# Second bias of 48 experts: spread over partitions ahead of the loop and added by VectorE, with token gathers issued an expert ahead

## The chip, the core and the metric

The kernel runs on one core of a Trainium2 chip. The core has five engines with queues of their own: PE (TensorE, matmuls and transposes), DVE (VectorE), ACT (ScalarE), POOL (GpSimd) and SP (SyncE, which here issues DMAs only). The metric is the device time of one execution in microseconds (us); of several runs the median is given.

## The reference, cut to what matters

The program is four layers deep, and each layer has an attention part and a feed-forward part. The change lies in the second layer's feed-forward part, a mixture of 48 experts over 4096 tokens of 256 numbers. Each expert picks the 128 tokens with its highest scores out of the 4096 tokens; the batch is 8 sequences of 512.

```python
E, S, D, M = (48, 4, 256, 256)
K = D // S
...
logits = xf @ Wr.T
vals, idx = jax.lax.top_k(logits.T, cap)          # cap = 128
w = jax.nn.softmax(vals, axis=-1)
xg = xf[idx]
h = jax.nn.gelu(jnp.einsum('ecd,esdm->ecsm', xg, W1) + b1[:, None], approximate=False)
y = jnp.einsum('ecsm,esmk->ecsk', h, W2) + b2[:, None]
y = y.reshape(E, cap, D) * w[..., None]
out = jnp.zeros_like(xf).at[idx.reshape(-1)].add(y.reshape(-1, D))
```

`b2` is the second bias: one row of 256 numbers for each expert, the same for all of its 128 tokens.

## The kernel before, in words

Activations stay in SBUF as `X`, 8 sequences of 4 x 128 tokens with the tokens on partitions. The part in question is the function `l1_ffn` (line 1326 on); it follows `l1_attn` and uses the helper class `Choice`.

**The gap.** The routing of seven sequences is done during the attention part. What is left when the attention of the eighth sequence ends can't be hidden. `finish` of `l1_attn` ends with the output projection (L193), its norm (`stats`, L105 to L96, and L170 on DVE, L177 on ACT) and the addition to `X` (L182 on POOL). Then `ch.logits(7)` takes the norm of that sequence (L105 to L133, DVE), stores it in DRAM (`xn_d`, L1156), transposes it (L146), copies it (L148) and multiplies by the router's weights (L1165, L1170). `ch.lists(4)` sorts: 16 rounds of MAX8, FIND_INDEX8 and MATCH_REPLACE8 on DVE (L1183 to L1188), and stores the table (L1195, SP). `ch.slots` merges all lists on DVE, reads windows of the table with five indirect DMAs (L1277, POOL) and ends with the tokens' indices `iT` and weights `wT` for all experts.

**The loop.** For each expert `e`: SP loads `w1` (1 MB, L1350), `w2` (256 KB, L1351) and the row `b2` (1 KB, L1352), each with three buffers; POOL gathers the 128 tokens (L1354, two buffers); PE transposes them (L1359) and DVE copies them to `xgT` (L1361). PE multiplies by `w1` (L1368, 32 instructions, since each float32 matmul is two), ACT takes the gelu with the first bias (L1373, 8 instructions). The second stage accumulates in one PSUM tile `py`: first a matmul of a row of ones with the row `b2` (L1377, two instructions), which puts the bias on all 128 rows, then eight matmuls of 64 columns (L1379, 16 instructions) on top of it. DVE weights the result (L1383), and POOL adds it to the tokens' rows in DRAM with an indirect DMA (L1384).

**The order.** Each engine works through its queue in order and waits at an instruction until what it needs is there. The order of each queue is fixed when the program is built, by the framework's own estimate of when things are ready; it need not be the order of the text. So the profile has the transposes L1359 and the bias matmul L1377 of the next expert between the L1379 of this one, and weight loads of the first three experts ahead of the table's store on SP.

Of the kernel before, what the change touches and what calls it, by code (L numbers as in the profile page):

```python
# [9 lines left out]
F32 = mybir.dt.float32  # L10
# [4 lines left out]
ALU = mybir.AluOpType  # L15
# [4 lines left out]
P = 128  # L20
NB = 8
L = 512
NT = 4
D = 256
# [1080 lines left out]
class Choice:  # L1105
# [7 lines left out]
    E, NL, K = 48, 10, 128  # L1113
# [212 lines left out]
def l1_ffn(K):  # L1326
    nc, tc = K.nc, K.tc
    b1 = K.W["l1_ffn"][:, 96:480]
    ch, i = K.choice, K.i
    E = ch.E  # L1330
    with ExitStack() as es:
        es.enter_context(ch.es)

        def pool(name, bufs, **kw):
            return es.enter_context(tc.tile_pool(name="f1" + name, bufs=bufs, **kw))
        cst = pool("c", 1)
        wp = pool("w", 3)
        sb = pool("s", 2)
        pmm = pool("pm", 2, space=PSUM)
        pH = pool("ph", 4, space=PSUM)  # L1340
        pY = pool("py", 2, space=PSUM)
        ch.logits(NB - 1, sb, pmm, "mm")
        for _ in ch.lists(len(ch.GROUPS) - 1):
            pass
        wT, iT = ch.slots(cst, sb, pmm, "mm")
        for e in range(E):
            w1 = wp.tile([P, 4, 2, D], F32, tag="w1", name=f"w1_{e}")
            w2 = wp.tile([P, 4, 2, 64], F32, tag="w2", name=f"w2_{e}")
            b2 = wp.tile([1, D], F32, tag="b2", name=f"b2_{e}")
            nc.sync.dma_start(out=w1, in_=i["l1f_w1"][e].rearrange("s (c p) m -> p s c m", p=P))  # L1350
            nc.sync.dma_start(out=w2, in_=i["l1f_w2"][e].rearrange("s (c p) k -> p s c k", p=P))  # L1351
            nc.sync.dma_start(out=b2, in_=i["l1f_b2"][e:e + 1, :])  # L1352
            xg = sb.tile([P, D], F32, tag="xg", name=f"xg{e}")
            nc.gpsimd.indirect_dma_start(  # L1354
                out=xg, out_offset=None, in_=ch.xn_d[:, :],
                in_offset=bass.IndirectOffsetOnAxis(ap=iT[:, e:e + 1], axis=0))
            ps = pmm.tile([P, 2, P], F32, tag="mm", name=f"pxg{e}")
            for c in range(2):
                nc.tensor.transpose(ps[:, c, :], xg[:, c * P:(c + 1) * P], K.ident)  # L1359
            xgT = sb.tile([P, 2, P], F32, tag="xgT", name=f"xgT{e}")  # L1360
            nc.vector.tensor_copy(xgT, ps)  # L1361
            hT = sb.tile([P, 8, P], F32, tag="hT", name=f"hT{e}")
            for half in range(2):
                ph = pH.tile([P, 4, P], F32, tag="h", name=f"h{e}_{half}")
                for j in range(4):
                    s, m = 2 * half + j // 2, j % 2
                    for c in range(2):
                        nc.tensor.matmul(  # L1368
                            ph[:, j, :], lhsT=w1[:, s, c, m * P:(m + 1) * P],
                            rhs=xgT[:, c, :], start=(c == 0), stop=(c == 1))  # L1370
                for j in range(4):
                    q = 4 * half + j
                    nc.scalar.activation(  # L1373
                        hT[:, q, :], ph[:, j, :], AF.Gelu,
                        bias=b1[:, 8 * e + q:8 * e + q + 1])
            py = pY.tile([P, D], F32, tag="y", name=f"y{e}")
            nc.tensor.matmul(py, lhsT=K.ones, rhs=b2, start=True, stop=False)  # L1377
            for q in range(8):
                nc.tensor.matmul(  # L1379
                    py[:, (q // 2) * 64:(q // 2 + 1) * 64], lhsT=hT[:, q, :],  # L1380
                    rhs=w2[:, q // 2, q % 2, :], start=False, stop=(q == 7))
            yw = sb.tile([P, D], F32, tag="yw", name=f"yw{e}")
            nc.vector.tensor_scalar(yw, py, wT[:, e:e + 1], None, ALU.mult)  # L1383
            nc.gpsimd.indirect_dma_start(  # L1384
                out=ch.out_d[:, :],
                out_offset=bass.IndirectOffsetOnAxis(ap=iT[:, e:e + 1], axis=0),
                in_=yw, in_offset=None, compute_op=ALU.add)

    def late(b, pool):
        y = pool.tile([P, NT, D], F32, tag="xn", name=f"yl{b}")  # L1390
        nc.sync.dma_start(
            out=y, in_=ch.out_d[b * L:(b + 1) * L].rearrange("(n p) d -> p n d", p=P))
        K.add_norm(b, [y[:, n, :] for n in range(NT)], pool, parts=2)


    K.late = late
# [847 lines left out]
def l3_ffn(K):  # L2244
# [18 lines left out]
    with ExitStack() as es:  # L2263
# [295 lines left out]
        for b in range(NB):  # L2559
# [11 lines left out]

LAYERS = (("l0_attn", load_l0_attn, l0_attn), ("l0_ffn", load_l0_ffn, l0_ffn),
          ("l1_attn", load_l1_attn, l1_attn), ("l1_ffn", load_l1_ffn, l1_ffn),
          ("l2_attn", load_l2_attn, l2_attn), ("l2_ffn", load_l2_ffn, lambda K: None),
          ("l3_attn", load_l3_attn, l3_attn), ("l3_ffn", lambda K: None, l3_ffn))
# [94 lines left out]
```

## Time and profile before

| what | value |
|---|---|
| median of 3 runs | 4563.06 us (4558.62 to 4568.67) |
| profiled execution | 4555.24 us |
| its span, first to last instruction | 4553.5 us |
| mean granted PE clock | 0.93 of full speed |
| PE busy | 3963.8 us, 87% of the span |
| DVE busy | 2698.8 us, 59% |
| POOL busy | 2118.9 us, 47% |
| ACT busy | 2016.2 us, 44% |
| end of the last L193 of the attention to the first L1359 of the experts | 1513.8 to 1577.1 us |
| first L1359 to the last L1383 of the experts | 1577.1 to 1882.0 us |

How to read the lines: a line of the timeline has the start and the duration in us, the engine, the line of the source, the operation, the output and the inputs by the program's names, partitions x elements, and how many instructions were merged into it; in brackets stands how long the engine was idle before and what ended that. Buffer numbers are left out of names, so `y` is `y0`, `y1` and so on. PEld is PE's loading of weights, which lies beside its matmuls. SPq is an instruction that only issues a DMA. The clock is a share of full speed.

### The profile page before, as it was taken

Reading aid. Unit: us, or ns where it says so; the run is one execution under the profiler, and the core shown is the slowest. Engines: PE = TensorE matmul, PEld = TensorE weight load, DVE = VectorE, ACT = ScalarE, POOL = GpSimd, SP = SyncE. Lnnn points to the kernel's source line nnn. Section 1 sums busy time; section 2 is a strip of 40 time slices with the busy share of each in tenths; the row PEclk is TensorE's granted clock in tenths of the full one; section 3 lists DMA queues with packets and bytes.
Section 4 is the critical chain, followed back from the end, with each engine's and each line's share of the span. In section 5 each row is a group of like instructions: output and inputs, shape, how many; then the busy total and the mean of one; then the engine's idle time right before and its main releaser. Section 6 shows DMA issues by size and latency. Waiting matters only on the chain. (4 is left out here: it accounts for less than half of the span.)

```text
span 4553.5 us, 63426 instructions
## 1 busy us (share of the span) xinstructions
PE 3963.8 (87%) x21672; PEld 2633.7 (58%) x21672; DVE 2698.8 (59%) x7145; ACT 2016.2 (44%) x4210; POOL 2118.9 (47%) x2081
## 2 busy tenths in 40 slices
PE   8868888999998599699999978998888876899997
PEld 3435765555655499544554534565655545678884
DVE  7767656456757611255566534888888899721115
ACT  5532433444344233334444444767676655311112
POOL 0045222444344244344555423889988879223321
PEclk9889999999999799889999989899999886899999
DMA  4377621000000299400000002343433334336653
GB/s 120 94 218 189 179 62 63 5 5 7 7 10 16 69 254 251 130 5 10 6 6 6 1 23 68 123 125 126 127 122 122 124 110 136 103 118 234 228 180 113
DMA packets 392818, 442.90 MB, mean 97 GB/s; under 512 B 147853, under 2 KB 275967, under 8 KB 391983
## 3 DMA queue, kind: packets, MB, share of 16 engines
q1 hardware_dynamic: 361087, 390.18, 28.4%
q0 software_dynamic: 16272, 31.87, 2.6%
q10 hardware_dynamic: 15136, 16.80, 1.1%
q8 instruction: 172, 2.82, 0.3%
q14 instruction: 151, 1.24, 0.1%
HBM read 372.49 MB, written 66.26 MB: 96 GB/s over the span
## 5 line engine op out<-in xcount | busy, mean ns | idle before, releaser
L2085 POOL TENSOR_TENSOR h<-h,C 128x1024 f32<-128x1024 f32 x256 | 613.3, 2408 | 135.3 <-DVE h L2081 87.8
L2081 DVE TENSOR_TENSOR_SCAN h<-dA,dB 128x512 f32<-128x512 f32 x480 | 568.4, 1209 | 90.2 <-ACT dA L2069 73.9
L1039 POOL TENSOR_SCALAR p<-p,rs 128x128 f32<-128x128 f32 (+3 forms) x256 | 275.8, 1085 | 417.3 <-DVE rs L1038 261.1
L2069 ACT ACTIVATE dA<-dl,A 128x512 f32<-128x512 f32 x480 | 330.3, 690 | 174.4 <-DVE h L2081 173.7
L1605 DVE CUSTOM_DVE_ANT_0 junk<-S,mask 128x256 f32<-128x256 f32 (+3 forms) x512 | 249.5, 487 | 195.0 <-PE S L1599 156.7
L2098 PE MATMUL y<-C,h 128*128 128x128 f32 x2048 | 298.4, 297 | 68.0 <-POOL h L2085 67.9
L2098 PEld LDWEIGHTS y<-C,h 128*128 128x128 f32 x2048 | 263.2, 155 | 155.3 <-POOL h L2085 98.6
L1633 ACT ACTIVATE PT<-T 128x128 f32<-128x128 f32 (+3 forms) x512 | 198.0, 435 | 278.5 <-PE T L1628 267.6
L1599 PE MATMUL S<-KZ,QT 64*128 64x512 f32 (+3 forms) x1024 | 260.9, 492 | 23.9 <-DVE mx L1605 23.6
L2297 PE MATMUL gb<-xbT,w_b 128*128 128x256 f32 (+1 forms) x1472 | 255.3, 332 | 1.0 <-ACT ts L2501 0.6
L2297 PEld LDWEIGHTS gb<-xbT,w_b 128*128 128x128 f32 x1472 | 230.4, 191 | 22.8 <-ACT ts L2501 0.8
L2303 DVE TENSOR_TENSOR hTb<-sb,gb 128x512 f32<-128x512 f32 x71 | 48.8, 687 | 325.4 <-PE gb L2297 325.4
L2064 POOL TENSOR_TENSOR dB<-du,B 128x1024 f32<-128x1024 f32 x96 | 234.0, 2437 | 0.1
L1883 PE MATMUL pf<-fT,w_l_ffn 128*128 128x512 f32 x384 | 208.3, 681 | 26.5 <-ACT fT L1877 10.4
L1628 PE MATMUL T<-QT,KZ 64*128 64x384 f32 (+3 forms) x1024 | 216.7, 464 | 2.9 <-ACT PT L1633 2.5
L2064 DVE TENSOR_TENSOR dB<-du,pb 128x1024 f32<-128x1024 f32 x160 | 191.2, 1195 | 23.0 <-ACT pb L2062 21.2
L182 POOL TENSOR_TENSOR X<-X,yn 128x256 f32<-128x256 f32 (+1 forms) x56 | 79.4, 1436 | 255.3 <-ACT yn L177 213.9
L1373 ACT ACTIVATE hT<-h,w_l_ffn 128x128 f32<-128x128 f32 x384 | 109.5, 368 | 197.9 <-PE h L1368 197.9
L1368 PE MATMUL h<-xgT,w 128*128 128x128 f32 x1536 | 185.0, 279 | 0.0
L1636 POOL TENSOR_SCALAR_AFFINE_SELECT PT<-PT 128x512 f32<-128x512 f32 x128 | 81.2, 634 | 219.8 <-ACT PT L1633 206.8
L1599 PEld LDWEIGHTS S<-KZ,QT 64*128 64x128 f32 x1024 | 117.2, 193 | 113.9 <-issue 58.4
L2534 POOL DMA_INDIRECT ys<-yb,place x71 | 69.8, 984 | 238.7 <-ACT yb L2533 224.5
(605 smaller groups left out, 9266.5 us busy)
## 6 DMA issues: line engine op xcount, KB each, us to landing
w_b<-l3f_w SPq DMA_DIRECT2D x138, 512.0 KB
C<-xdd SPq DMA_DIRECT2D x256, 256.0 KB
B<-xdd SPq DMA_DIRECT2D x256, 256.0 KB
w<-l1f_w SPq DMA_DIRECT2D x48, 1024.0 KB
w<-l1f_w SPq DMA_DIRECT2D x48, 256.0 KB
band<-l0fd SPq DMA_DIRECT2D x30, 320.0 KB
X<-x SPq DMA_DIRECT2D x16, 512.0 KB
c<-ys SPq DMA_DIRECT2D x16, 512.0 KB
```

The source lines that it names most:

```text
L1039: nc.gpsimd.tensor_scalar(p[:, 0:n], p[:, 0:n], rs, None, ALU.mult)
L1599: nc.tensor.matmul(ps[:, 0:n], lhsT=QT[half, qt * P:n], rhs=KZ[half, j % 2, 0:n], start=True, stop=True)
L1605: nc.vector.tensor_tensor_reduce(out=junk[:, 0:n], in0=ps[:, 0:n], in1=mask[:, L - n:L], scale=1.0, scalar=-3.0e38, op0=ALU.add, op1=ALU.m ...
L1628: nc.tensor.matmul(ps[:, 0:n], lhsT=KZ[half, j % 2, kt * P:(kt + 1) * P], rhs=QT[half, kt * P:L], start=True, stop=True)
L1633: nc.scalar.activation(PT[:, j, :], ps[:, 0:n], AF.Exp)
L1883: nc.tensor.matmul(ps, lhsT=gu[:, k, j * 768 + c * P:j * 768 + (c + 1) * P], rhs=R[b]["fT"][:, k, :], start=(k == 0), stop=(k == 1))
L2064: on.tensor_tensor(dBs[k], R[b]["du", h], B[:, None, :].to_broadcast([P, 2, L]), ALU.mult)
L2069: nc.scalar.activation(dA, R[b]["dl", h][:, c, :], AF.Exp, scale=A[:, 2 * h + c, n:n + 1])
L2081: nc.vector.tensor_tensor_scan(hs[k][:, c, :], dA, dBs[k][:, c, :], 0.0, ALU.mult, ALU.add)
L2085: nc.gpsimd.tensor_tensor(hs[k], hs[k], row_C.pop(k)[:, None, :].to_broadcast([P, 2, L]), ALU.mult)
L2098: nc.tensor.matmul(R[b]["y", h][q // 2][:, q % 2, c * P:(c + 1) * P], lhsT=t[:, c, q * P:(q + 1) * P], rhs=K.ident, is_transpose=True, sta ...
L2297: nc.tensor.matmul(ps[:, q, :], lhsT=ww[:, k, (c + q) * P:(c + q + 1) * P], rhs=xT[:, k, :], start=(k == 0), stop=(k == 1))
```

## The change

The second bias leaves the accumulation. In the gap all 48 rows are loaded with experts on partitions (48 x 256). For each pair of experts POOL multiplies the rows with two columns of the identity, which leaves only the own row of each expert in a block of 48 x 512; a matmul with a 48 x 128 tile of ones sums over the 48 rows and so puts the pair's rows on all 128 partitions, and ACT copies them to the tile `bb` in SBUF (48 KB on each partition). The scratch for the product takes the buffers of `w2`. In the loop the eight matmuls start their own sums, and DVE adds `bb` before it weights. The gather of expert `e + 1` is now issued, in the text, before the work on expert `e`, with three buffers instead of two. `ch.logits` of the last sequence takes its tiles from a pool that is closed again before the loop.

```diff
-        ch.logits(NB - 1, sb, pmm, "mm")
+        bb = cst.tile([P, E, D], F32, name="bb")
+        with ExitStack() as eg:
+            sg = eg.enter_context(tc.tile_pool(name="f1g", bufs=1))
+            b2 = sg.tile([E, D], F32, name="b2")
+            nc.sync.dma_start(out=b2, in_=i["l1f_b2"])
+            ch.logits(NB - 1, sg, pmm, "mm")
+            one = sg.tile([E, P], F32, name="one")
+            nc.gpsimd.memset(one, 1.0)
+            for e in range(0, E, 2):
+                own = wp.tile([P, 4, 2, 64], F32, tag="w2", name=f"own{e}")
+                own = own[0:E].rearrange("p a b k -> p (a b k)").rearrange("p (m d) -> p m d", m=2)
+                nc.gpsimd.tensor_tensor(
+                    own, b2[:, None, :].to_broadcast([E, 2, D]),
+                    K.ident[0:E, e:e + 2, None].to_broadcast([E, 2, D]), ALU.mult)
+                pb = pH.tile([P, 2, D], F32, tag="h", name=f"pb{e}")
+                nc.tensor.matmul(pb, lhsT=one, rhs=own, start=True, stop=True)
+                nc.scalar.copy(bb[:, e:e + 2, :], pb)
...
+        xgs = {}
+
+        def gather(e):
+            xgs[e] = sb.tile([P, D], F32, tag="xg", name=f"xg{e}", bufs=3)
+            nc.gpsimd.indirect_dma_start(
+                out=xgs[e], out_offset=None, in_=ch.xn_d[:, :],
+                in_offset=bass.IndirectOffsetOnAxis(ap=iT[:, e:e + 1], axis=0))
+
+        gather(0)
         for e in range(E):
...
-            b2 = wp.tile([1, D], F32, tag="b2", name=f"b2_{e}")
...
-            nc.sync.dma_start(out=b2, in_=i["l1f_b2"][e:e + 1, :])
-            xg = sb.tile([P, D], F32, tag="xg", name=f"xg{e}")
-            nc.gpsimd.indirect_dma_start(
-                out=xg, out_offset=None, in_=ch.xn_d[:, :],
-                in_offset=bass.IndirectOffsetOnAxis(ap=iT[:, e:e + 1], axis=0))
+            if e + 1 < E:
+                gather(e + 1)
+            xg = xgs.pop(e)
...
-            nc.tensor.matmul(py, lhsT=K.ones, rhs=b2, start=True, stop=False)
             for q in range(8):
                 nc.tensor.matmul(
                     py[:, (q // 2) * 64:(q // 2 + 1) * 64], lhsT=hT[:, q, :],
-                    rhs=w2[:, q // 2, q % 2, :], start=False, stop=(q == 7))
+                    rhs=w2[:, q // 2, q % 2, :], start=(q % 2 == 0), stop=(q % 2 == 1))
             yw = sb.tile([P, D], F32, tag="yw", name=f"yw{e}")
-            nc.vector.tensor_scalar(yw, py, wT[:, e:e + 1], None, ALU.mult)
+            nc.vector.tensor_tensor(yw, py, bb[:, e, :], ALU.add)
+            nc.vector.tensor_scalar(yw, yw, wT[:, e:e + 1], None, ALU.mult)
```

## The prediction

> **What bounds the kernel now.** I read the page first and found no one bound: the engines' shares change from stage to stage. So I went to the two stages that the change touches, by a table of windows (the columns after the window's length are PE, PEld, DVE, ACT and POOL busy with instruction counts, granted clock, DMA share, GB/s), then the timeline in each, then the waits.
>
> ```profile
> 1514.00:1577.00 63.00, 11.54 (x40) 8.94 (x39) 43.93 (x182) 8.68 (x18) 9.65 (x11) 0.56 0.14 41
> ...
> 1650.00:1700.00 50.00, 50.00 (x415) 46.38 (x414) 6.98 (x16) 18.24 (x64) 20.34 (x16) 1.00 0.95 249
> ```
>
> The first line is the gap: routing of the last sequence, one chain that runs mostly on DVE; PE, ACT, POOL and the DMA are nearly idle. The second is the expert loop: PE is never idle, at full clock. So in the gap only what delays DVE's chain costs, and in the loop only PE's queue counts. The timeline of one loop period shows that queue:
>
> ```profile
> 1722.47 1.23 PE L1379 MATMUL y<-w,hT 128*128 128x64 f32 x10
> 1722.66 0.37 SPq L1350 DMA_DIRECT2D w<-l1f_w  x1
> 1722.67 1.14 ACT L1373 ACTIVATE hT<-h,w_l_ffn 128x128 f32<-128x128 f32 x4 [0.58 <-PE h L1368]
> ...
> 1723.53 0.28 PE L1359 MATMUL pxg<-C,xg 128*128 128x128 f32 x1
> ...
> 1723.82 0.28 PE L1359 MATMUL pxg<-C,xg 128*128 128x128 f32 x1
> ...
> 1724.02 0.69 PE L1377 MATMUL y<-b,ones 1*128 1x256 f32 x2
> 1724.13 0.42 DVE L1361 COPY xgT<-pxg 128x256 f32<-128x256 f32 x1 [4.60 <-PE pxg L1359]
> ...
> 1724.65 0.66 PE L1379 MATMUL y<-w,hT 128*128 128x64 f32 x4
> ...
> 1725.14 3.79 PE L1368 MATMUL h<-xgT,w 128*128 128x128 f32 x32
> ```
>
> Read: the transposes of the next expert's tokens and its bias matmul (L1377) already stand among this expert's y matmuls. h starts at 1605.40, 1611.70, 1618.01 and so on: a period of 6.30 us.
>
> **Part 1, the bias matmul leaves the loop.** L1377 holds PE from 1724.02 to 1724.65, when the next y starts: 0.63 us. Without it the last four y instructions run 1724.02 to 1724.51 (their 0.49 us). What is late next is xgT: its copy starts when the second transpose ends and is done at 1724.13 + 0.42 = 1724.55. With a hop of about 0.07 (estimate; the copy itself starts 0.03 after the transposes) h starts at 1724.62 and not 1725.14: 0.52 us per expert. The gelu does not bind: its last four end at 1723.81, before the y matmuls that read them. 47 periods x 0.52 = **24.4 us gained**. From above it is the whole 0.63: 29.6 us. From below it is less than nothing, if the build orders PE's queue otherwise (rival C).
>
> Could the DMA, at 0.95, become the bound? Its share is not flat: in slices of 0.3 us it carries w1 at about 380 GB/s, then w2 at 180 to 290, and falls to 0.06 to 0.6 for some 1.5 us of each period. The prefetch of three experts ran in 12.7 us (1504.7 to 1517.4), 4.2 us each; gather and scatter come on top, 1.44 us per expert if the software queue's 18.0% of 16 engines in 1500 to 1885 is put end to end. That is 5.7 at most, against a period of 5.78. It stays hidden.
>
> **Part 2, DVE's added instruction.** y is read from PSUM by an addition (nearest: 128x256 of L889, two operands and one of them PSUM, 0.42) and then weighted from SBUF (L133's 0.35), in place of 0.48. DVE has 7 us of work in 50, and the scatter has slack: POOL waits 3 us per period. So nothing in the loop, some 0.3 us once behind the last expert, and 0.3 for reordered starts: +0.6.
>
> **Part 3, the gather an expert ahead.** At 1604.63 the gather is issued right after the transposes that freed its buffer; with two buffers that is already the tokens of two experts on, used 11 us later, and it lands in 4.2 us. PE waited for a gather twice in all, 4.1 us, at the start. Gain: nothing. The 48 loads of one row that leave SP's queue freed nothing anyone waited for.
>
> **Part 4, the spreading in the gap.** Added: a load of 48 KB, a memset, 24 POOL products of 48x512, 24 pairs of matmul instructions of 512 columns, 24 ACT copies of 128x512. ACT: 24 x 0.58 = 13.9 us beside 8.7 busy in 63. PE: L193 does 256 columns in 0.22, so 24 x 2 x 0.44 = 21 us beside 11.5 busy. POOL: rows with a spread operand of 512 are L1587 at 1.04 and L1547 at 1.06, plain ones reach 1.27 (L1498) and 1.43 (L672); I take 1.1, so 24 x 1.1 = 26 us of POOL, idle from 1521 to the window gathers at 1564. By room alone all is free. The weights' buffers w2 serve as scratch, so w2 loads wait for the last product; even from 1550 on three experts' weights land in 12.7 us, before 1577, and the table store at 1553.29 has until 1564.
>
> But POOL and DVE are not independent:
>
> ```profile
> 748.01 2.35 POOL L182 TENSOR_TENSOR X<-X,yn 128x1024 f32<-128x1024 f32 x1 [6.00 <-ACT yn L177]
> 748.13 2.25 DVE L96 SCALAR_TENSOR_TENSOR ony<-onw,ony 128x4 f32<-128x4 f32 x1
> ```
>
> and, earlier, with two POOL products in a row:
>
> ```profile
> 446.99 1.27 POOL L903 TENSOR_TENSOR oT<-oT,ro 128x512 f32<-128x512 f32 x1 [0.34 <-ACT ro L901]
> 447.23 1.57 DVE L906 SCALAR_TENSOR_TENSOR oT<-sq,oT 128x512 f32<-128x512 f32 x1
> 448.21 2.80 POOL L762 TENSOR_TENSOR bq<-bq,PQ 128x1024 f32<-128x1024 f32 x1
> ```
>
> A 0.16 us DVE instruction on 128x4 takes 2.25 and ends with POOL's product, 20 ns after it. In the second view DVE's turn comes when POOL's instruction ends, and POOL's next one is longer. So while POOL runs products back to back, each DVE instruction with two SBUF inputs passes once per product. MAX8, FIND_INDEX8, BATCH_NORM_STATS2 and the like never stretched.
>
> Which are exposed: the root of the output norm (L94 to L96 three times each, L170: 10, at 1515.5 to 1517.4), that of the routing norm (9, at 1522.3 to 1524.0) and the four L133 (1524.1 to 1525.5; L133's longest is 2.46, so it is held too). Products can't start before the bias rows are in and PSUM is free; L1377 of the first experts ran at 1513.77, so I start there. Some three products go before X's additions, which interrupt POOL until about 1521; about 18 are left, 20 us in a row, over the whole second chain. 13 exposed instructions x (1.1 - 0.2) = 11.7; for the first chain 3 x 0.9 = 2.7, taken at half, 1.3, since the start is uncertain. Transposes and copies of the chain queue behind the spreading's own on PE and ACT: +1. In return PE is kept warm: the clock was 0.50 from 1518.75 to 1528.5 and L1165 took 3.03 for 8 instructions of 256 columns, 1.8 at L193's pace, and the 8 transposes would give some 0.8: -2. **Gap: 11.7 + 1.3 + 1 - 2 = +12.** Lower end -2 (products fall under the 20 us of MAX8 and its like); upper end 28 (24 products of 1.27 each charged, less 24 x 0.2, and two more ahead of X's additions).
>
> [...]
>
> **Sum** on the profiled execution (4555.24, span 4553.5): -24.4 + 0.6 + 12 = -11.8, 4543.4. The median of the runs shown is 7.8 above it, 4563.06; the same difference gives **4551**.
>
> **Rivals.**
> A, the gap is nearly free (-2 to +6): the products start late or are spread out so that they fall under MAX8. For it: 20 us of MAX8 and its like with POOL empty. Against: they are ready earlier and POOL takes them as soon as it can. Time: about 4541.
> B, the gap is dear (+17 to +28): nearly every product holds one DVE instruction, or POOL's queue has products ahead of X's additions. For it: 23 exposed two-input and L133 instructions, 24 products. Against: X's additions stop POOL in between. Time: about 4562.
> C, **slower**: a wait replaces the bias matmul. It was one of the fillers that PE's queue had while hT was late; reordered, the two transposes may stand behind the last y. Then transposes (0.40), copy (0.45) and hop (0.07) lie bare: 3.63 (h) + 16 x 0.12 (y) + 0.92 = 6.47 a period, 0.17 over now, 47 x 0.17 = +8, and with the gap +21: 4584. It decides where the second transpose ends less than 0.5 us before the last y; today it is 1.0. Against it: xg is there early, so nothing pushes the transposes back.
>
> **Chances.** Forecast (gap +7 to +16) 0.48, 4546 to 4555; A 0.20; B 0.20; C 0.12. A measurement here can tell 0.2%, 9.1 us, from no change: 4554. Faster: most of the forecast, 0.38, and A: 0.58. Same: 0.10 and B: 0.30. Slower: C, 0.12. The range runs from A with part of the 0.63 (4534) to B's end (4567) and leaves out C and a little of A.
>
> **What would show it.** Right: an h period near 5.78, h starting just after xgT's copy; in the gap, 24 POOL products near 1.1 us and L94 to L96 and L133 near 1 us each instead of 0.16 and 0.35, the first MAX8 some 12 us later than the 17 us it now has after PE's last L193. Wrong: PE idle before h by more than 0.2 us; products above 1.5 us; L94 to L96 unchanged; the window gathers waiting for POOL's products and not for DVE.

## The result and the profile after

The kernel after takes 4571.17 us (median of 15 runs, 4565.81 to 4577.77), the kernel before 4562.82 us (15 runs). The ratio is 1.0016, with a 95% interval of 1.0009 to 1.0023: slower by 0.16%; the two medians lie 8.4 us apart. 4551 was predicted, 11.8 us faster.

For the comparison the span is cut into four: *upstream* ends at the start of the last L193 matmul of the attention, the *gap* goes from there to the first transposition of `pxg`, the *loop* from there to the first instruction of the next stage (which waits for the last scatter's landing), *downstream* is the rest. `after_again` is a second profile of the same kernel after (4576.62 us): the first, 4565.81 us, was the quickest of its 15 runs.

| us | before | after | after_again |
|---|---|---|---|
| upstream | 1513.5 | 1517.7 | 1515.1 |
| gap | 63.6 | 73.9 | 73.5 |
| loop | 312.0 | 309.6 | 318.8 |
| downstream | 2664.4 | 2662.9 | 2667.5 |
| span | 4553.5 | 4564.1 | 4574.9 |
| scatter, median from issue to landing | 3.9 | 5.2 | 6.1 |

The trace of `after_again` has the landing of 24 of the 48 scatters only, those of `gather_only` and `wide_products` below of 37; the others have 47 or 48.

The gap is 10 us longer, as forecast (+12). The loop, which was to give 24 us, gives 2.4 in one profile and takes 6.8 in the other. Upstream and downstream moved by 1.6 to 4.2 and by -1.5 to 3.1 us, and not alike in the two profiles.

Three windows of after: the gap, the first 50 us of the loop at full pace, and the next 50 (columns as in the prediction).

```profile
1514.00:1592.00 78.00, 54.44 (x105) 26.66 (x103) 50.50 (x182) 22.48 (x42) 35.49 (x36) 0.58 0.24 70
1610.00:1660.00 50.00, 50.00 (x449) 49.66 (x449) 9.71 (x24) 20.50 (x73) 20.18 (x16) 1.00 1.04 274
1660.00:1710.00 50.00, 46.53 (x402) 45.77 (x401) 10.31 (x26) 18.25 (x65) 22.38 (x17) 0.97 0.98 255
```

In the second row PE is never idle and does 449 instructions (415 before): the pace that was hoped for, and more. In the third it does 402 and stands idle for 3.5 us. Something takes hold some 70 us into the loop and does not let go. The waits of after from 1591 to 1891 us say what (what waited, what it waited for, us in all, times, longest), and below them the scatter's wait in before:

```profile
POOL out_d L1406 <- DVE yw L1404: 134.4, 38, 7.5
DVE yw L1404 <- DMA out_d<-yw,iT: 126.3, 35, 6.8
```

```profile
POOL out_d L1384 <- DVE yw L1383: 55.2, 48, 8.2
```

In before VectorE never waited for a scatter, and POOL's scatter waited 55 us for `yw`. Now VectorE's add waits 35 times for the landing of an earlier scatter, because that scatter still reads the `yw` buffer that the add is to fill.

### The profile page after: what moved, and what is told of

Same layout as the page of the kernel before. It is cut to its first block, busy times and chain, and to the rows that moved or that the text cites. A ratio compares the mean times of both kernels' runs of the same rounds, so it can differ in the third digit from the quotient of the medians.

```text
span 4564.1 us, 63312 instructions
## 1 busy us (share of the span) xinstructions
PE 3979.8 (87%) x21624; PEld 2642.3 (58%) x21624; DVE 2714.2 (59%) x7193; ACT 2030.9 (44%) x4234; POOL 2149.4 (47%) x2106
## 5 line engine op out<-in xcount | busy, mean ns | idle before, releaser
L2103 DVE TENSOR_TENSOR_SCAN h<-dA,dB 128x512 f32<-128x512 f32 x480 | 568.3, 1208 | 89.8 <-ACT dA L2091 73.5
L1905 PE MATMUL pf<-fT,w_l_ffn 128*128 128x512 f32 x384 | 210.1, 686 | 26.3 <-ACT fT L1899 10.5
L1390 PE MATMUL h<-xgT,w 128*128 128x128 f32 x1536 | 202.8, 288 | 0.1
L1390 PEld LDWEIGHTS h<-xgT,w 128*128 128x128 f32 x1536 | 189.3, 201 | 0.8 <-DVE xgT L1383 0.2
```

The source lines that it names most:

```text
L1390: nc.tensor.matmul(ph[:, j, :], lhsT=w1[:, s, c, m * P:(m + 1) * P], rhs=xgT[:, c, :], start=(c == 0), stop=(c == 1))
L1905: nc.tensor.matmul(ps, lhsT=gu[:, k, j * 768 + c * P:j * 768 + (c + 1) * P], rhs=R[b]["fT"][:, k, :], start=(k == 0), stop=(k == 1))
L2103: nc.vector.tensor_tensor_scan(hs[k][:, c, :], dA, dBs[k][:, c, :], 0.0, ALU.mult, ALU.add)
```

## The experiments

Eleven kernels. The table has what the profile of each shows; the time is the median with the number of runs, and the ratio is to runs of before made beside them. Where there is one run, its gap and its loop are compared, and not its total.

| kernel | time, us | ratio to before (95%) | gap | loop | landing |
|---|---|---|---|---|---|
| gather_only | 4561.49 (10) | 1.0001 (0.9992 to 1.0010) | 64.0 | 311.6 | 4.4 |
| bias_only | 4567.86 (5) | 1.0032 (1.0015 to 1.0049) | 74.1 | 304.4 | 5.4 |
| unpaired | 4564.76 (11) | 1.0003 (0.9994 to 1.0013) | 73.6 | 306.1 | 5.4 |
| two_sums | 4543.23 (5) | 0.9963 (0.9950 to 0.9976) | 77.2 | 278.1 | 5.5 |
| bias_by_dma | 4565.22 (10) | 1.0003 (0.9994 to 1.0012) | 63.1 | 318.2 | 5.6 |
| wide_products | 4566.73 (1) | | 67.2 | 311.8 | 5.5 |
| before_two_sums | 4559.17 (1) | | 63.4 | 311.8 | 4.0 |
| two_sums_merged | 4533.66 (5) | 0.9936 (0.9923 to 0.9950) | 64.1 | 278.2 | 5.5 |
| three_weights | 4535.74 (1) | | 73.8 | 279.0 | 3.9 |
| four_yw | 4560.57 (1) | | 63.2 | 313.1 | 5.4 |
| merged_unpaired | 4546.07 (1) | | 64.0 | 288.7 | 5.3 |

### Which part, and is it the order?

The order in which a program's instructions are recorded changed along with the edit: without the bias matmul the loop goes in pairs of experts (both experts' transpositions together, two gathers, then two scatters on POOL). My first theory, ORDER, was that the pairs cost what the matmul gave. Three kernels test it.

`gather_only` is before with the gathers of after, `bias_only` is after with the gathers of before:

```diff
+            xgs[e] = sb.tile([P, D], F32, tag="xg", name=f"xg{e}", bufs=3)
...
+            if e + 1 < E:
+                gather(e + 1)
+            xg = xgs.pop(e)
```

> The kernel before, with one edit of the change alone: the tokens of the next expert are gathered an expert ahead (three xg buffers); the bias matmul stays in the loop. In the recorded order the loop still goes one expert at a time (scatter, gather, scatter, gather on POOL). Loop means first transposition of pxg to the end of the last scatter: 312.0 us before, 309.6 after. Theory ORDER (without the bias matmul the recording orders the loop in pairs of experts, and the pairs cost what the matmul gave): this order is unpaired, loop 310 to 313, gap 73 to 75, total within 0.1% of before. Rival GATHER (the earlier gather itself holds the scatters up on POOL's queue): loop 325 to 335, total slower by 0.3 to 0.5%. Rival FILL (the DMA engines are full below 6.1 us per expert, whatever the order): loop 310 to 313 as well.

> The kernel after with the gathers put back where the kernel before has them (two xg buffers, the gather just ahead of its expert); everything else of the change stays. The recorded order of the loop is in pairs of experts as in after (two gathers, two scatters; both experts' transpositions together). Theory ORDER: loop 307 to 312 as in after (309.6), gap 83 to 85, total as after within 0.1%. Rival GATHER: the loop falls to 288 to 294, total about 20 us below after. Rival FILL: loop 307 to 312.

`unpaired` adds to after an edge that orders PE's queue and waits for nothing:

```diff
                 t = nc.tensor.transpose(ps[:, c, :], xg[:, c * P:(c + 1) * P], K.ident)
+                if last is not None:
+                    behind(t, last)       # last: the previous expert's last h matmul
```

> The kernel after with one thing added: an ordering edge without a semaphore puts each expert's transpositions behind the last h matmul of the expert before it. With it the recorded order is one expert at a time, as in the kernel before, less the bias matmul (POOL: scatter, gather, scatter, gather). Theory ORDER: loop 287 to 294 us (312.0 less 47 matmuls of 0.4 to 0.52 us), gap 83 to 85 as in after, total 4545 to 4555, faster than before by 0.2 to 0.4%. Rival FILL: loop 307 to 312, period still 6.1 to 6.2 us and the DMA engines at 1.0, total as after. Rival GATHER: loop 307 to 312.

Measured: the gathers alone do nothing (loop 311.6 against 312.0). `bias_only` has the loop at 304.4, a few us below what ORDER gave it and far above the 288 to 294 of GATHER. In `unpaired` the old order is back and the loop is 306.1, not 287 to 294: ORDER falls. But `unpaired` shows the mechanism better than any other kernel. VectorE early in its loop, where each copy to `xgT` begins an expert:

```profile
1614.20 0.42 DVE L1390 COPY xgT<-pxg 128x256 f32<-128x256 f32 x1 [4.48 <-PE pxg L1386]
1620.02 0.42 DVE L1390 COPY xgT<-pxg 128x256 f32<-128x256 f32 x1 [4.48 <-PE pxg L1386]
1625.84 0.42 DVE L1390 COPY xgT<-pxg 128x256 f32<-128x256 f32 x1 [4.49 <-PE pxg L1386]
1631.66 0.42 DVE L1390 COPY xgT<-pxg 128x256 f32<-128x256 f32 x1 [4.49 <-PE pxg L1386]
```

and POOL's scatters of the same time:

```profile
1617.33 1.58 POOL L1413 DMA_INDIRECT out_d<-yw,iT  x1 [1.90 <-DMA out_d<-yw,iT]
...
1623.39 1.56 POOL L1413 DMA_INDIRECT out_d<-yw,iT  x1 [2.15 <-DMA out_d<-yw,iT]
...
1630.63 1.57 POOL L1413 DMA_INDIRECT out_d<-yw,iT  x1 [3.56 <-DMA out_d<-yw,iT]
...
1637.57 1.57 POOL L1413 DMA_INDIRECT out_d<-yw,iT  x1 [4.07 <-DMA out_d<-yw,iT]
```

PE starts an expert every 5.82 us (6.30 before). The scatters start 6.06, 7.24 and 6.94 us apart, each 0.8 us after the one before it has landed: they all add into one tensor, different experts can have the same token, and so each must wait for the last. The scatters fall behind by 2.8 us in three experts. Later in the same loop the lag has used up the two `yw` buffers:

```profile
1776.94 0.42 DVE L1411 TENSOR_TENSOR yw<-y,bb 128x256 f32<-128x256 f32 x1 [5.17 <-DMA out_d<-yw,iT]
...
1777.61 1.58 POOL L1413 DMA_INDIRECT out_d<-yw,iT  x1 [5.57 <-DVE yw L1411]
1777.67 0.42 DVE L1390 COPY xgT<-pxg 128x256 f32<-128x256 f32 x1
1778.14 3.84 PE L1397 MATMUL h<-xgT,w 128*128 128x128 f32 x32 [0.62 <-DVE xgT L1390]
...
1782.78 0.42 DVE L1411 TENSOR_TENSOR yw<-y,bb 128x256 f32<-128x256 f32 x1 [4.70 <-DMA out_d<-yw,iT]
...
1783.46 1.58 POOL L1413 DMA_INDIRECT out_d<-yw,iT  x1 [2.97 <-DVE yw L1411]
```

One landing releases two things at once: VectorE's add, which needs its buffer, and POOL's next scatter, which holds an expert finished long before. (The line of 1783.46 names VectorE as what POOL waited for; the landing that released VectorE was the one that POOL needed too.) `xgT` stands behind the add on VectorE, and PE's `h` behind `xgT`. The period is now the landing plus 0.8 us: the scatter of 1777.61 lands 5.1 us later, VectorE's add starts at 1782.78, and the next scatter 0.68 after that.

In after the same chain reaches PE by another way:

```profile
1669.30 1.58 POOL L1406 DMA_INDIRECT out_d<-yw,iT  x1 [6.51 <-DVE yw L1404]
...
1672.51 0.98 POOL L1366 DMA_INDIRECT xg<-xn_d,iT  x1 [0.30 <-issue]
...
1676.30 0.33 PE L1381 MATMUL pxg<-C,xg 128*128 128x128 f32 x1 [2.82 <-DMA xg<-xn_d,iT]
```

The two gathers of the next pair stand behind the held scatter on POOL's queue, and PE waits for the tokens. From 1602 us on PE is idle for 17.1 us in the loop of after, 17.0 of them before `pxg`. After its last transposition the last scatter starts 18.6 us later (12.5 in `two_sums`, below), and the granted clock of 1610 to 1850 us is 0.97 (1.00 in before).

### Is it the chain of scatters, or the DMA as a whole?

`two_sums` cuts the chain in two:

```diff
+        self.out_o = K.dram.tile([NB * L, D], F32, name="out_o")     # zeroed like out_d
...
-                out=ch.out_d[:, :],
+                out=(ch.out_o if e % 2 else ch.out_d)[:, :],
```

> The kernel after, but the odd experts' scatters go to a second tensor that starts at zero, so that a scatter waits only for the landing of the one two before it. The odd experts' part is left out of the sum that follows. The recorded order stays in pairs. One more zeroing transfer of 4 MB stands early in the program. Theory SERIAL (the chain issue, landing, next issue of scatters into one tensor sets the period of after): the wait of VectorE's add and of the scatters falls, loop 285 to 300. Rival FILL (DMA full): loop 307 to 312 with the DMA engines still at 1.0 and scatters landing later. Rival PE ORDER (the pairs' order of matmuls on TensorE itself leaves PE idle, waiting for gathers or gelu): loop 303 to 312, with PE's idle time put down to xg or hT and not to yw.

`before_two_sums` is the same edit in the kernel before.

> The kernel before, with the odd experts' scatters going to a second tensor that starts at zero (their part is left out of the sum that follows). Theory SERIAL says that the chain of scatters became the limit only when the bias matmul had left TensorE: in before, TensorE was busy in 50.0 of 50 us, so a shorter chain gives nothing here; loop 308 to 313 us (312.0 before). Rival (the chain of scatters had set the period already): loop 285 to 300.

Measured: 278.1 us in after and 311.8 in before (312.0 uncut). Cutting the chain is worth 31 us (41 against the second profile of after) where the bias matmul is gone, and nothing where it stands. The scatters of `two_sums` land no sooner (5.5 us); they only have to wait less often for it. The rivals fall: 278.1 is far from the 303 to 312 of FILL and PE ORDER, and though `two_sums` has the pairs of after, PE waits for nothing from 1600 to 1880 us. Its gap is 3 us longer than that of after; why stays open.

`three_weights` leaves the chain whole and takes away the traffic beside it:

```diff
-            nc.sync.dma_start(out=w1, ...)      # and w2, for every expert
+            if e < 3:
+                ...                             # tiles and loads as before, kept in held
+            w1, w2 = held[e % 3]
```

> The kernel after, but only the weights of the first three experts are loaded; the later experts use those three sets again, so 45 of the 48 experts compute with the wrong weights, and some 56 MB of loads leave the loop. Scatters stay in one tensor and in one chain. Theory SERIAL, with the landing stretched by the weights' traffic: a scatter lands 3.7 to 4.2 us after its issue in place of 5.2 (median of after), so the chain (landing and 0.7 us to the next start) needs under 5 us, TensorE sets the pace at 5.6 us, and the loop is 276 to 284 us. Rival (a landing is stretched by the gathers beside it, or by the chain itself): landing 5 us or more and a loop above 295.

The loop is 279.0. The landings of the scatters, in before, in after and in three_weights (least, median, most, us):

```profile
DMA to landing us min/median/max: 3.7/3.9/5.8
```

```profile
DMA to landing us min/median/max: 3.8/5.2/8.4
```

```profile
DMA to landing us min/median/max: 3.7/3.9/5.7
```

So a scatter takes 3.9 us where no weights are loaded beside it and 5 to 6 in after, where they are: the weights' traffic stretches the landing, and not the gathers or the chain. How busy the DMA engines are on average does not say by how much. In before they were busy 0.95 of the time (1600 to 1850 us) and a scatter landed in 3.9; in `bias_by_dma` 0.89 (1685 to 1845 us) and it landed in 5.6. What differs is when a scatter is issued. In before 42 of the 44 scatters that fall between loads start 0.77 us after the issue of `w2`'s load, for instance at 1707.20 after 1706.43, and the next load of `w1` is issued at 1710.06; the queue of the weights then fills 0.49 of the engines from 1 to 4 us after the scatter's start, on average. In after a scatter starts 0.2 to 4.7 us after the last load of weights, and the share is 0.68; in `bias_by_dma` it is 0.83. That the place of the scatter among the loads sets its landing is argued from this, and not shown: no run moved it by itself.

`four_yw` asks whether the two buffers are the cause. It is `bias_by_dma` (below) with `bufs=4` for `yw`.

> The kernel bias_by_dma with four buffers for yw in place of two, so that VectorE's add waits for the landing of the scatter four before it. Theory SERIAL: the scatters still follow one another landing by landing, so the loop stays at 302 to 320 us (318.2 in bias_by_dma, 309.6 in after) and only the wait moves, from VectorE's add to POOL's scatter. Rival BUFFERS (two yw buffers are what makes VectorE wait, and the copies of xgT behind it): loop 278 to 292.

Loop 313.1 (318.2 with two buffers), and the wait moved to where SERIAL put it: POOL's scatter waited 30 times, 120 us, for an earlier landing. More buffers move the wait; they do not shorten a chain.

> The kernel after unchanged, for a second profile: how far the loop moves from one execution to the next. Theory SERIAL: the loop is a sum of 48 landings that differ between 3.8 and 8.4 us, so it moves by several us, between 304 and 320 (309.6 in the first profile), while the gap stays at 73 to 75.

318.8 us, with landings of 6.1: of the 10.8 us between the two profiled executions of after, 9.2 lie in the loop. A loop that is a sum of landings is also a loop that varies; where PE sets the pace, in before, `gather_only` and `before_two_sums`, the loops lie between 311.6 and 312.0.

### What makes the gap longer?

`bias_by_dma` fills `bb` by one transfer, with no work on POOL, PE or ACT:

```diff
-            for e in range(0, E, 2):            # products, matmuls and copies
-                ...
+            nc.sync.dma_start(out=bb, in_=i["l1f_b2"].partition_broadcast(P))
```

> The kernel after, but bb is filled by one transfer that repeats the second bias on all partitions (6.3 MB into on-chip memory) in place of the 24 products on POOL, the 24 matmuls and the 24 copies on ScalarE. Loop and its order as in after. Gap here means last py of the stage before to the first transposition of pxg: 63.6 and 64.0 us without the spreading (before, gather_only), 73.6 to 74.1 with it (after, bias_only, unpaired). Theory SPREAD (the three engines' work for the spreading makes the gap longer): gap 63 to 66, loop 304 to 311, total 8 to 10 us below after. Rival MEMORY (the room that bb takes lets w1 and the first gathers start late, whoever fills it): gap 72 to 75, total as after.

Gap 63.1: the spreading is the whole of the 10 us. The loop came out at 318.2, beyond the 304 to 311 expected; the loop of after moved as far between its two profiles.

In after the products start at 1525.3, when X's additions are over, and hold instructions of the second norm, as forecast, but fewer:

```profile
1525.89 0.43 DVE L118 TENSOR_SCALAR lnv<-lnmv 128x4 f32<-128x4 f32 x1
1526.35 0.96 DVE L90 TENSOR_SCALAR lny<-lnv 128x4 int32<-128x4 int32 x1
...
1527.35 0.96 DVE L91 TENSOR_SCALAR lny<-lny 128x4 int32<-128x4 int32 x1
1528.35 0.16 DVE L94 TENSOR_TENSOR lnw<-lnh,lny 128x4 f32<-128x4 f32 x1
1528.54 1.01 DVE L95 TENSOR_TENSOR lnw<-lnw,lny 128x4 f32<-128x4 f32 x1
...
1530.37 0.89 DVE L94 TENSOR_TENSOR lnw<-lnh,lny 128x4 f32<-128x4 f32 x1
```

Five are held, for 3.4 us: L118, L90, L91, L95 and one L94, each 0.16 or 0.17 in before. L118, L90 and L91 are 128x4 TENSOR_SCALARs, which the sum does not count; elsewhere in before L118 took up to 0.93 us, L90 2.03 and L91 2.32, each of these ending 0.03 us after a product of POOL. The others pass because POOL soon waits for PE, 0.7 us before the product of 1530.20 and 5.3 before the next. That is what I had not seen coming:

```profile
1532.16 2.30 PE L146 MATMUL pxT<-C,xn 128*128 128x128 f32 x8 [2.04 <-DVE xn L133]
1534.39 2.07 PE L1357 MATMUL pb<-own,one 48*128 48x512 f32 x2
1536.39 3.78 PE L1165 MATMUL pl<-xT,wz 128*128 128x256 f32 x8
1540.10 2.07 PE L1357 MATMUL pb<-own,one 48*128 48x512 f32 x4
```

A spreading pair stands between the chain's transpositions and its router matmul, and PE runs at half clock (0.50 granted in 1532.2 to 1536.4 us and in 1536.4 to 1540.1): a pair of spreading matmuls takes 1.7 to 2 us where 0.88 was reckoned. So the products run until 1569, past the last MAX8, and hold the merge as well: L1191 takes 0.99 us (0.23 before), the 14 of L1218 take 5.02 (2.66 before). Counted from the last L193, the first MAX8 is 6.1 us later than before, the first window gather 9.8, the first transposition 10.3.

`wide_products` changes only the number of rows that the spreading contracts:

```diff
-            b2 = sg.tile([E, D], F32, name="b2")
+            b2 = sg.tile([P, D], F32, name="b2")          # rows 48 to 127 zero
...
-            one = sg.tile([E, P], F32, name="one")
+            one = sg.tile([P, P], F32, name="one")
```

> The kernel after, but the products and the matmuls that spread them use all 128 partitions as contraction rows (rows 48 to 127 of the bias are zero) in place of 48. In after, TensorE stood busy in 54 of 77 us of the gap with these 48-row matmuls, yet the granted clock fell to 0.5 and one matmul of 512 columns took 0.85 us in place of 0.43. Theory ROWS (few rows count as little work for the clock): the matmuls stay at 0.43 us, the clock of the gap rises from 0.58 to 0.8 or more, and the gap falls from 73.9 to 68 to 72. Rival: the clock falls for another reason, such as the waits between matmuls; matmuls of 0.85 us again and a gap of 73 to 75.

The spreading matmuls in after, then in wide_products (shortest, median, longest in ns, first and last start):

```profile
L1357 PE MATMUL pb<-own,one x48: 589/1057/1219, 1526.3 to 1571.9; 48*128 48x512 f32 x48
```

```profile
L1358 PE MATMUL pb<-own,one x48: 592/593/1221, 1526.1 to 1557.5; 128*128 128x512 f32 x48
```

The granted clock (the last column but two) while PE is busy with them, in after, then in wide_products:

```profile
1540.00:1573.00 33.00, 32.94 (x43) 12.66 (x42) 30.33 (x105) 12.48 (x23) 18.61 (x18) 0.55 0.05 12
```

```profile
1540.00:1557.50 17.50, 17.50 (x37) 5.52 (x36) 16.60 (x64) 10.63 (x19) 16.92 (x17) 1.00 0.01 2
```

The gap falls to 67.2, just under the 68 to 72 expected: with the clock at 1.00, 6.7 of the 10.3 us are gone, so they came from the clock of 0.55 beside the 48-row matmuls. The other 3.5 are about the 3.4 by which the held norm ends later here too.

### A version that beats both

`two_sums_merged` is `bias_by_dma` with two sums, and the next stage adds them, so nothing is left out:

```diff
+            yo = s1.tile([P, NT, D], F32, tag="xn", name=f"yo{b}")
+            nc.sync.dma_start(
+                out=yo, in_=K.choice.out_o[b * L:(b + 1) * L].rearrange("(n p) d -> p n d", p=P))
+            nc.vector.tensor_tensor(y, y, yo, ALU.add)
```

> A version meant to beat both: bb by the one transfer, odd experts' scatters into a second zeroed tensor, and nothing left out: the next stage loads both tensors and VectorE adds them (8 additions of 128x1024). Theory SERIAL with SPREAD: loop 276 to 281 us (278.1 in two_sums), gap 63 to 67, and 2 to 9 us more in the next stage for the second loads and the additions; total 4529 to 4541, faster than before by 0.5 to 0.7%. If DMA traffic were the limit of the loop, 304 to 311 and a total near before.

4533.66 us, 0.64% faster than before (0.50 to 0.77): gap 64.1, loop 278.2, downstream 2671.8 (7.4 above before, with eight additions of 1.22 us; profiles of kernels that leave this part alone lie from 1.5 below to 4.2 above before, so the merge costs some 3 to 9 us). A window in the loop:

```profile
1650.00:1700.00 50.00, 50.00 (x449) 49.65 (x449) 9.41 (x26) 20.58 (x72) 23.39 (x18) 1.00 1.08 284
```

PE is never idle, and the DMA carries 284 GB/s where before carried 249: its bandwidth was no limit there.

> The kernel two_sums_merged with the ordering edge of unpaired (each expert's transpositions behind the last h matmul of the expert before), to price the pairing by itself where the chain of scatters no longer limits. From the stretches in which TensorE set the pace: 5.82 us per expert unpaired, 5.59 paired. So the loop is 286 to 291 us (278.2 paired), and the total 8 to 12 us above two_sums_merged, 4540 to 4546. If the recorded order makes no difference once the chain is broken: 276 to 281.

Loop 288.7, time 4546.07: where the chain does not limit, the pairs gain 10.5 us. The order that I first blamed is an advantage.

## Why the prediction was wrong

**What bounds the kernel: right for before.** PE set the loop's period; `before_two_sums` confirms that no wait on scatters stood behind it. "In the loop only PE's queue counts" no longer holds in after.

**Part 1: the gain was right, and out of reach.** 0.52 us per expert was forecast; `unpaired`, while PE sets its pace, goes from 6.30 to 5.82, 0.48 per expert. "It stays hidden" holds for the bandwidth of the DMA, which `two_sums_merged` drives to a period of 5.59 us. Both were sums of work. Neither looked at how long a transfer takes to land.

**Part 2 is the step that failed: "the scatter has slack: POOL waits 3 us per period. So nothing in the loop."** Those 3 us are POOL's wait before the gather, for the buffer that PE still reads (44 times, 127.1 us); they are no measure of the scatters' slack. What counts is the chain from landing to landing. In before a landing took 4.3 us on average (median 3.9) and the hop to the next scatter needs 0.8: 5.1 us against a period of 6.30. The slack was 1.2 us in a period that was to shrink by 0.5, and the rise of the landing to 5.4 took the rest: 6.2 us in the chain against 5.78 forecast. The scatters of after started 6.25 us apart on average, in the second profile 6.44. The loop's -24.4 + 0.6 became -2.4 and +6.8.

**Part 3: right.** The earlier gather alone is worth nothing (1.0001).

**Part 4: the size was right, its make-up was not.** +12 was forecast, +10.3 and +9.9 measured. No product ran ahead of `X`'s additions, so the 1.3 for the first norm was nothing, and the four L133 were not held. The 13 held instructions at 0.9 were 5 in the norm, 3.4 us; "PE is kept warm: -2" went the other way, since with the 48-row matmuls the clock was 0.55 (1.00 with 128 rows), and the products stretched over the merge, 6.7 us. Products of 1.1 us were 1.03.

**Rivals.** C had the right kind of cause, a wait in place of the matmul, at the wrong place: PE's order, which in fact improved. Had only the gap been off, the forecast would have been within 2 us; the loop came out 21 and 31 us above its forecast of -23.8.

## What to carry to other kernels

Before counting on a shorter loop, list its chains of dependent transfers, add issue to landing for one turn, and compare that with the new period and not with the old. Leave room for the landing to grow: a landing read in the old loop (3.9 us here) need not hold in the new one (5.2 and 6.1). Where several transfers add into one tensor, a second tensor and one addition at the end can be worth far more than a faster engine: here 31 us of the loop, for 3 to 9 us of merging, where the shorter queue of PE with one sum gave at most 7.6 (`bias_only`). An engine's idle time does not tell the latency of what it issues: POOL waited 3 us a period in before, with landings of 3.9.

## What the runs showed of the hardware that was not expected

- A busy PE was not always a PE at full clock. In after, PE was busy for 32.9 of the 33 us from 1540 to 1573 with 48-row matmuls at a granted clock of 0.55; with 128 rows, 80 of them zero, the clock was 1.00 and a matmul instruction took 593 ns in place of 1057. So the number of rows made the difference here; by what rule, no run shows.
- An accumulating scatter of 128 rows lands in 3.9 us where no weights are loaded beside it (`three_weights`), and beside the same loads in 3.9 (before) or in 5.2 to 5.6 (after, `bias_by_dma`). The mean share of the DMA engines does not tell which: it was 0.95 in before and 0.89 in `bias_by_dma`.
